# Two single PSUM banks as tiles of their own in the first sweep of a graph layer

## The chip, the cores and the metric

The kernel runs on one core of a Trainium2 chip. TensorE (PE in the profile, its weight loads PEld) multiplies into PSUM; VectorE (DVE) and ScalarE (ACT) read and write PSUM and SBUF; GpSimd (POOL) works in SBUF; SyncE (SP) issues the transfers. The metric is the device time of one execution in microseconds, as a median of several.

## The reference

For each of 64 batches there is a 256 x 768 block `x` and a 256 x 256 matrix `adj` of zeros and ones. With `h` the normalised and rectified `x`:

```
h    = max(layernorm(x), 0)
ctx  = adj @ (h @ Wadj.T) / deg  +  adj.T @ (h @ Wrev.T) / rdeg  +  h @ Wself.T      (biases left out)
rel  = (adj-weighted sums of E rows) @ Wr.T  +  the same, reversed, @ Wrr.T
out  = x + ctx + rel
```

So three products of a 256 x 768 by a 768 x 768 matrix are needed in each batch, in fp32 accuracy, and then two products with the adjacency matrix. As the entries are zeros and ones, the part `rel` comes down to a few rows added per batch.

## The kernel before

The three dense products of a batch are computed as one product of a block matrix through 15 smaller products (a scheme with fewer multiplications; the table `PRODUCTS` names them 1 to 15). Each factor is a sum or difference of column blocks of `h`, named `a0` to `b2`. To keep fp32 accuracy in TensorE's faster format, a left factor is split into three words: `left0` (ACT, line 593), `left1` (DVE, line 606) and `left2` (DVE, line 610). Weights are split alike and stay in SBUF. All 15 sets of weights don't fit there at once, so there are two sweeps over the batches: the first does products 10, 5, 2, 8, 11, 14, 3 and 13, writes its partial sums and `h` to memory, and the second does the other seven, the adjacency products and the output. Two of the 64 batches take a direct path with plain fp32 matmuls (`whole`, line 763).

A product accumulates in a chain of PSUM: in the first sweep the chains are `y`, `z` and `w`. `product` (line 627) records for each the first group of matmuls (line 621), a rescaling by ACT in place (line 655), the second group of matmuls, and reads of the sum by ACT (line 666) or DVE (lines 675 and 677). Four matmuls per word pair, 12 per product, 96 per batch in this sweep.

Nothing is issued as it is recorded. Each step is an operation with an engine, an estimated cost and a rank (a due time with a hand-set offset from a table), and `Plan.schedule` (line 301) plays the engines through in time, gives each buffer a slot of its class and writes out one order for all. `main_path` (line 1049) then emits that order. A buffer becomes a tile when its first operation is emitted: the pool, and a tag made of class and slot. A new tile under a tag waits for those that used the one before it.

[...]Class `Q` has four slots of two banks. One `Q` buffer, `hold` (line 451), lives through the whole first sweep, and its two halves, one bank each, are the two slots of class `U`. A `U` buffer is used for three things:

- `top` (line 597): in the first sweep, ACT copies `left0` of a product into it (line 600), and DVE reads it for `left1` (line 606) and `left2` (line 610). Eight a batch.
- `pt` (line 705): TensorE transposes the row statistics into it (line 707) and ACT reads them as `line` (line 710), which goes to memory and back as the broadcast `row` with which POOL (line 726) and DVE (line 730) normalise `h`. One a batch, two batches ahead.
- `right` (line 488): at the start, the weights of product 3 are summed by TensorE in it (line 495) and split into words by ACT and DVE. Four in all.

A `U` buffer gets no tile; it is a view of half of `hold`'s tile:

```
for b in sorted(o.bufs, key=lambda b: bool(b.inside)):
    if b.inside:
        b.tile = b.inside.tile[:, b.slot, :]
```

With `hold` in place the chains share the other three slots of `Q`: a batch's `y` takes the slot that the `z` of the batch before it leaves, once DVE has read `z` (line 677, `x<-z`, product 2's sum). After the first sweep the slot of `hold` is used like the others.

Of the kernel before, what the change touches and what calls it, by code (L numbers as in the profile page):

```python
# [10 lines left out]
F32 = mybir.dt.float32  # L11
# [6 lines left out]
P = 128  # L18
# [221 lines left out]
class Buf:  # L240
    def __init__(self, cls, shape, dtype, name):
        self.cls, self.shape, self.dtype, self.name = cls, shape, dtype, name
        self.ops, self.parts, self.slot, self.tile, self.inside = [], {}, None, None, None


class Op:
# [765 lines left out]
def kernel(  # L1012
# [36 lines left out]
    def main_path(main: ExitStack):  # L1049
        pool = main.enter_context(tc.tile_pool(name="pool", bufs=1))  # L1050
        dram = main.enter_context(tc.tile_pool(name="dram", bufs=3, space=bass.MemoryType.DRAM))
        keep = main.enter_context(tc.tile_pool(name="kept", bufs=1, space=bass.MemoryType.DRAM))
        psum = main.enter_context(tc.tile_pool(name="psum", bufs=1, space=bass.MemoryType.PSUM))
        plan = Plan(SLOTS)
        own = lambda name, shape, dtype: plan.buf(None, shape, dtype, name, pool.tile(shape, dtype, name=name))
        fixed = {
            "x": x_v, "xt": x_t, "adj": adj_v, "out": out_v, "e_t": e_t, "bias": bias,
            "w": (wadj_t, wself_t, wrev_t), "wr": (wr_t, wrr_t),
            "ident": ident, "ones": ones, "half": half, "dram": dram, "kept": keep,
            "flag": plan.buf(None, None, None, "flag", flag),  # L1060
            "deg": own("deg", [P, B, C, 2], F32),
            "sq": own("sq", [P, B, C], F32),
            "cols": [own(f"cols{i}", [P, P], F32) for i in range(2)],
            "halves": [[own(f"half{c}_{i}", [P, P], F32R) for c in range(C)] for i in range(2)],
            "rd": [own(f"rd{i}", [P, C, 2], F32) for i in range(2)],
        }
        for col in fixed["cols"]:
            nc.vector.memset(col.tile, 0.0)
        for half_tile in fixed["halves"][0] + fixed["halves"][1]:
            nc.vector.memset(half_tile.tile.bitcast(F32), 0.0)  # L1070
        nc.scalar.activation(half[:, :1], half[:, :1], AF.Copy)
        record(nc, plan, fixed, B, NREL)
        for o in plan.schedule():
            for b in sorted(o.bufs, key=lambda b: bool(b.inside)):
                if b.inside:
                    b.tile = b.inside.tile[:, b.slot, :]
                elif b.tile is None:
                    b.tile = (psum if b.cls == "Q" else pool).tile(b.shape, b.dtype, tag=f"{b.cls}{b.slot}", name=b.name)
            o.emit()

    def general_path(sub: ExitStack):
# [121 lines left out]
    with ExitStack() as main:  # L1203
        with tc.manual_schedule():
            main_path(main)
# [37 lines left out]
```

## Time and profile before

| what | us |
|---|---|
| median of 3 executions | 2551.55 |
| lowest, highest | 2549.71, 2552.49 |
| the profiled execution: its own time | 2551.01 |
| the profiled execution: span from first to last instruction | 2549.2 |
| busy PE, PEld | 2509.0, 2408.4 |
| busy DVE, ACT, POOL | 2134.0, 1824.7, 1300.0 |

The share of busy time speaks for the whole span; the two sweeps must be read apart. A view by windows gives busy times of a stretch. A view of waits lists which instruction stood idle until which other was done, with the total, the times and the longest. A timeline lists instructions by start and length; what stands in brackets is the time for which the engine had been idle and who ended that. A line number with the tile name is the way to find a step in the code: `hold` in a row is a half of that tile, without saying which.

### The profile page before, as it was taken

To read this page: it belongs to the slowest core of one execution; us is meant where nothing else is said; L and a number is where in the kernel's file an instruction comes from. 1 tells how busy PE (TensorE), PEld (TensorE's weight loads), DVE (VectorE), ACT (ScalarE), POOL (GpSimd) and SP (SyncE) were. 2 spreads that over 40 slices of the span, in tenths; PEclk is the share of its full clock that TensorE was granted. 3 is DMA by queue.
4 is the path that set the end of the run, shared out by engine and by line. 5 is a ranking of instruction groups with operands and counts; after the bars stand their busy time and mean duration, and the time that the engine had idled before them with its cause. 6 is when DMAs were issued, how large, how long until landed. Compare 5 with 4: busy or idle time off the path is not lost. (4 is left out here: it accounts for less than half of the span.)

```text
span 2549.2 us, 43499 instructions
## 1 busy us (share of the span) xinstructions
PE 2509.0 (98%) x13922; PEld 2408.4 (94%) x13922; DVE 2134.0 (84%) x3933; ACT 1824.7 (72%) x3901; POOL 1300.0 (51%) x1138
## 2 busy tenths in 40 slices
PE   7999999999999999999999999999999999999998
PEld 4899999999999999996999999999999999999998
DVE  7777777777777777778899999999999999999997
ACT  4788888888888888886666666666666666666664
POOL 1555555555555555542555555555555555555553
PEclk9999999999999999999999999999999999999999
DMA  5677677777777777777576666676666666666663
GB/s 210 233 275 265 254 277 262 256 277 257 262 277 261 256 279 262 269 256 253 177 217 210 210 209 212 210 216 208 212 210 211 210 212 210 212 210 211 217 211 132
DMA packets 223970, 590.63 MB, mean 232 GB/s; under 512 B 24036, under 2 KB 24292, under 8 KB 223736
## 3 DMA queue, kind: packets, MB, share of 16 engines
q1 hardware_dynamic: 223736, 587.79, 68.3%
q8 instruction: 112, 1.84, 0.3%
q14 instruction: 122, 1.00, 0.1%
HBM read 364.22 MB, written 223.48 MB: 231 GB/s over the span
## 5 line engine op out<-in xcount | busy, mean ns | idle before, releaser
L903 POOL TENSOR_TENSOR hl<-c,hl 128x768 fp32r<-128x768 f32 x256 | 490.5, 1936 | 397.7 <-ACT hl L899 344.8
L621 PE MATMUL y<-word,left 128*128 128x384 f32 x2976 | 591.1, 340 | 12.1 <-DVE x L677 7.6
L621 PE MATMUL x<-word,left 128*128 128x384 f32 x2976 | 570.7, 336 | 1.5 <-ACT x L655 1.0
L621 PEld LDWEIGHTS y<-word,left 128*128 128x128 f32 x2976 | 518.7, 188 | 40.0 <-DVE x L677 28.5
L621 PEld LDWEIGHTS x<-word,left 128*128 128x128 f32 x2976 | 520.9, 188 | 4.7 <-ACT x L655 1.6
L915 PE MATMUL agg<-hl,a 128*128 128x384 f32 x2048 | 399.0, 338 | 0.1
L915 PEld LDWEIGHTS agg<-hl,a 128*128 128x128 f32 x2048 | 355.9, 188 | 15.2 <-DVE c L677 14.7
L726 POOL TENSOR_TENSOR h<-h,row 128x768 f32<-128x768 f32 x128 | 235.6, 1861 | 221.5 <-DMA row<-d 179.7
L899 ACT ACTIVATE hl<-c 128x768 fp32r<-128x768 f32 x256 | 203.2, 839 | 155.1 <-PE agg L915 142.8
L621 PE MATMUL w<-word,left 128*128 128x384 f32 x1488 | 304.2, 339 | 0.1
L621 PE MATMUL z<-word,left 128*128 128x384 f32 x1488 | 301.4, 337 | 0.4 <-ACT left L593 0.2
L610 DVE SCALAR_TENSOR_TENSOR left<-left,hold 128x256 fp32r<-128x256 f32 x496 | 201.2, 416 | 107.9 <-ACT hold L600 103.2
L926 DVE SCALAR_TENSOR_TENSOR c<-agg,rd,c 128x768 f32<-128x768 f32 x252 | 254.0, 1008 | 28.7 <-PE agg L915 28.5
L610 DVE SCALAR_TENSOR_TENSOR left<-left 128x256 fp32r<-128x256 f32 x434 | 267.9, 640 | 0.0
L655 ACT ACTIVATE x<-x 128x768 f32<-128x768 f32 x248 | 197.4, 796 | 96.2 <-PE x L621 94.6
L621 PEld LDWEIGHTS z<-word,left 128*128 128x128 f32 x1488 | 260.1, 188 | 4.0 <-ACT c L666 0.5
L621 PEld LDWEIGHTS w<-word,left 128*128 128x128 f32 x1488 | 258.3, 188 | 3.2 <-ACT c L666 0.4
L655 ACT ACTIVATE y<-y 128x768 f32<-128x768 f32 x248 | 197.1, 795 | 51.9 <-PE y L621 51.3
L600 ACT ACTIVATE hold<-left 128x256 f32<-128x256 f32 x496 | 191.2, 385 | 37.2 <-DVE left L610 15.4
L704 POOL TENSOR_TENSOR cols<-cols,half 128x2 f32<-128x2 f32 x64 | 82.7, 1292 | 213.6 <-DVE cols L703 210.4
L675 DVE TENSOR_TENSOR c<-c,v 128x768 f32<-128x768 f32 x124 | 117.9, 951 | 81.2 <-PE v L645 79.4
L583 POOL TENSOR_TENSOR a1+a<-h 128x256 f32<-128x256 f32 x62 | 45.9, 741 | 271.8 <-DMA h<-kept_h 239.7
(137 smaller groups left out, 4438.7 us busy)
## 6 DMA issues: line engine op xcount, KB each, us to landing
c<-kept SPq DMA_DIRECT2D x316, 384.0 KB
kept<-c SPq DMA_DIRECT2D x252, 384.0 KB
x<-in_x_dram SPq DMA_DIRECT2D x128, 384.0 KB
h<-in_x_t_dram SPq DMA_DIRECT2D x128, 384.0 KB
out_dram<-c SPq DMA_DIRECT2D x126, 384.0 KB
kept_h<-h SPq DMA_DIRECT2D x124, 384.0 KB
h<-kept_h SPq DMA_DIRECT2D x124, 384.0 KB
adj<-in_adj_dram SPq DMA_DIRECT2D x64, 512.0 KB
```

The costliest lines, as they stand in the source:

```text
L583: lambda: nc.gpsimd.tensor_tensor(t(home), x[1](), y[1](), op=op),
L600: lambda: nc.scalar.activation(view(top), t(w)[:, 0].bitcast(F32), AF.Copy),
L610: lambda: nc.vector.scalar_tensor_tensor(t(w)[:, 2], t(w)[:, 1].bitcast(F32), -STEP, first(), op0=ALU.mult, op1=ALU.add), s == 1,
L621: nc.tensor.matmul(t(q)[:, half, : H // 2], t(w)[:, lw, f, :], t(r[rw])[:, f, ts(half, H // 2)], start=start and i == 0 and f == 0, stop=s ...
L655: lambda: nc.scalar.activation(view(), view(), AF.Copy, scale=scale),
L675: emit = lambda to=to, op=op: nc.vector.tensor_tensor(to(), to(), view(), op=op)
L704: pool(0.7, r - 21.5, f"pow {b}", [col], [col], lambda: nc.gpsimd.tensor_tensor(var(), var(), v["half"], op=ALU.pow))
L726: lambda h=h, one=one: nc.gpsimd.tensor_tensor(t(h), t(h), one(0), op=ALU.subtract),
L899: lambda: nc.scalar.activation(t(pair)[:, 0], t(o), AF.Copy, scale=LOWER),
L903: lambda: nc.gpsimd.tensor_tensor(t(pair)[:, 1], t(o), t(pair)[:, 0].bitcast(F32), op=ALU.subtract),
L915: nc.tensor.matmul(t(q)[:, half, : H // 2], t(s["a"])[:, c, k, ts(ic, P)], t(pairs[c])[:, part, ts(half, H // 2)], start=(c == 0 and part ...
L926: lambda q=q, to=to, ic=ic: nc.vector.scalar_tensor_tensor(to(), t(q)[:, :, : H // 2], t(rd)[:, ic, k : k + 1], to(), op0=ALU.mult, op1=AL ...
```

## The change

`hold` no longer gets a tile. A `U` buffer has a shape of its own, one bank of fp32, and gets a tile in a new pool `single` under the tag of its slot, so two tags and two banks. The planner still keeps `hold` as a buffer that reserves one slot of `Q`. When the slot is handed to another `Q` buffer later on, `single` is closed and a pool `late` is opened for the buffers of that slot. The order of the operations, the slots and the ranks are those of before.

```diff
@@ class Buf
         self.cls, self.shape, self.dtype, self.name = cls, shape, dtype, name
         self.ops, self.parts, self.slot, self.tile, self.inside = [], {}, None, None, None
+        if cls == "U":
+            self.shape, self.dtype = [P, 512], F32
@@ main_path
         psum = main.enter_context(tc.tile_pool(name="psum", bufs=1, space=bass.MemoryType.PSUM))
+        singles = ExitStack()
+        single = singles.enter_context(tc.tile_pool(name="single", bufs=1, space=bass.MemoryType.PSUM))
+        held, late = None, None
...
         for o in plan.schedule():
-            for b in sorted(o.bufs, key=lambda b: bool(b.inside)):
-                if b.inside:
-                    b.tile = b.inside.tile[:, b.slot, :]
+            for b in o.bufs:
+                if b.name == "hold":
+                    held = b.slot
                 elif b.tile is None:
-                    b.tile = (psum if b.cls == "Q" else pool).tile(b.shape, b.dtype, tag=f"{b.cls}{b.slot}", name=b.name)
+                    home = {"Q": psum, "U": single}.get(b.cls, pool)
+                    if b.cls == "Q" and b.slot == held:
+                        if late is None:
+                            singles.close()
+                            late = main.enter_context(tc.tile_pool(name="late", bufs=1, space=bass.MemoryType.PSUM))
+                        home = late
+                    b.tile = home.tile(b.shape, b.dtype, tag=f"{b.cls}{b.slot}", name=b.name)
             o.emit()
```

## The prediction

> **What bounds the kernel now.** First the windows view, cut at 76 us (first product of the first sweep), 1150 us (its last) and 1202 us (first of the second). Columns: window, length, busy us (instructions) of PE, PEld, DVE, ACT and POOL, clock, DMA share, GB/s.
>
> ```profile
> 76.00:1150.00 1074.00, 1061.36 (x5966) 1027.54 (x5965) 823.82 (x1792) 886.61 (x1786) 571.44 (x553) 1.00 0.73 265
> 1202.00:2530.00 1328.00, 1326.45 (x7516) 1299.60 (x7515) 1201.45 (x1994) 866.86 (x1991) 695.40 (x555) 1.00 0.67 209
> ```
>
> TensorE carries both sweeps. In the first its weight loads (PEld) leave 46.5 us of 1074 idle; VectorE has 250 us free and ScalarE 187. So only what shortens PE's waits counts. Next, the waits view between 80 and 1150 us for PEld and for DVE (total, times, longest), and from the view of line 677 what its DVE reads waited for, of which the line on PE's `z` is shown:
>
> ```profile
> PEld y L621 <- DVE x L677: 28.5, 59, 0.8
> PEld y L621 <- DVE c L677: 6.2, 28, 0.2
> ...
> DVE left L610 <- ACT hold L600: 102.7, 122, 1.2
> ...
> DVE left L606 <- ACT line L710: 34.7, 59, 3.8
> DVE left L606 <- ACT hold L600: 28.7, 40, 2.3
> ...
>   PE z L621: 0.3, 1
> ```
>
> PE waits once per batch, 59 times, for DVE to read product 2's sum out of `z`: the next batch's `y` takes that pair of banks, because `hold` leaves the chains only three of the four slots. The read had to wait for PE's `z` only once. So it is ready and stands in DVE's queue behind other work: lines 610 and 606, which wait for ACT for 166 us in all. One such stretch in the timeline, DVE first, then ACT, then PE (start, length, engine, operation, in brackets the idle time before and its releaser):
>
> ```profile
> 628.72 0.42 DVE L606 TENSOR_TENSOR left<-h,hold 128x256 fp32r<-128x256 f32 x1 [0.67 <-ACT line L710]
> 630.32 0.42 DVE L610 SCALAR_TENSOR_TENSOR left<-left,hold 128x256 fp32r<-128x256 f32 x1 [1.18 <-ACT hold L600]
> 630.65 0.41 DVE L606 TENSOR_TENSOR left<-b0+b,hold 128x256 fp32r<-128x256 f32 x1
> 631.59 0.42 DVE L610 SCALAR_TENSOR_TENSOR left<-left,hold 128x256 fp32r<-128x256 f32 x1 [0.52 <-ACT hold L600]
> 631.92 0.95 DVE L677 SCALAR_TENSOR_TENSOR x<-z,x 128x768 f32<-128x768 f32 x1
> ```
>
> ```profile
> 628.43 0.25 ACT L710 ACTIVATE line<-hold 4x128 f32<-4x128 f32 x1
> ...
> 629.91 0.38 ACT L600 ACTIVATE hold<-left 128x256 f32<-128x256 f32 x1
> ...
> 631.16 0.39 ACT L600 ACTIVATE hold<-left 128x256 f32<-128x256 f32 x1 [0.18 <-DVE left L606]
> ```
>
> ```profile
> 629.75 1.57 PE L621 MATMUL z<-word,left 128*128 128x384 f32 x8
> ...
> 631.68 0.72 PEld L621 LDWEIGHTS y<-word,left 128*128 128x128 f32 x4
> 632.93 0.19 PEld L621 LDWEIGHTS y<-word,left 128*128 128x128 f32 x1 [0.53 <-DVE x L677]
> ```
>
> Read it with the halves that the planner hands out. Product 13 of a batch holds one half; the other holds product 14, then the transposed column `pt`, then product 5 of the next batch. The first 606 (left1 of 13) reads 13's half, written long before, yet starts 0.04 us after `line` has read the other half: a read held up by another read, of other data. The 610 behind it (left2 of 13) waits 1.18 us for ACT's copy of product 5 into the other half. The 610 at 631.59 (left2 of 5) waits 0.52 us for the copy of product 11, again into the half that it doesn't read. So the program orders accesses by the tile, not by the half. Of DVE's waits, 102.7 us (two a batch) and 34.7 us are of this false kind; the 28.7 are mostly true, left1 of 14 waiting for its own copy.
>
> **What the Trainium skill says.** "PSUM — Partial Sum Buffer", PSUM bank collisions raise a hardware error, asks for accesses to be guarded by bank and quadrant and lets engines use different banks at once. A half of `hold` is 512 fp32 wide, one such bank, so the halves need no order between them; the trace shows an order all the same. "Perfetto Trace Analysis", Identifying the Most-Contended Engine, judges TensorE by its weight loads rather than by matmul busy time; the trace agrees, since PE's matmul rows show 7.6 us of the same wait where the weight loads show 28.5. "SBUF — State Buffer", Who interferes with whom, says that a DVE instruction with two SBUF inputs contends with GpSimd. Agreed: line 610 with `hold` never exceeds 425 ns in 496 runs, while in the second sweep, without `hold`, the same operation reaches 2079.
>
> **The change part by part.** Ranks, slots and the order on each engine come from the planner, which is not touched: no instruction or DMA of the work is added, dropped or moved, and SP's and POOL's queues keep their order. What changes is which tile an access names.
>
> (a) Each `top`, `pt` and `right` gets a tile of its own in the pool `single`, one tag per half. The false waits go: DVE's two kinds above, and ACT's for line 606 (11.1 us, 59 times, by the same view). True ones stay: a copy waits until the last reader of its own slot is through.
>
> In the stretch shown, left1 and left2 of 13 would run from about 628.1, under the wait. Left1 of 5 inherits the true wait: its copy ends at 629.91 + 0.38 = 630.29, so it starts at 630.33 and not at 630.65. Left2 of 5 follows 0.46 later (the spacing of such a pair without a wait: 625.75 and 626.21 in the same view), at 630.79, and ends at 631.21. The `z` matmuls end at 629.75 + 1.57 = 631.32. DVE starts some 0.10 us after such an end (the `w` matmuls from 617.07 take 1.55, DVE reads them from 618.72), so the read runs from 631.42 to 632.37 in place of 631.92 to 632.87. It released PE 0.06 us after its end; that becomes 632.43. PE was free to load at 631.68 + 0.72 = 632.40. The wait shrinks from 0.53 to 0.03.
>
> Over the sweep: 28.5 / 59 = 0.483 us a batch, less about 0.05, the part of such a wait in PEld that does not move the matmuls (0.53 us idle there moved them by 0.49), is 0.433 x 59 = 25.6 us. The 6.2 us behind `c<-y` I leave in: there DVE stands behind the normalisation (line 730) and left1 of 14, whose wait is true.
>
> What is late next: PE itself, 96 matmuls at 0.174 us (8 in 1.39 from run to run) or 16.7 us a batch, some 0.12 for the transpose and 0.1 for `c<-y`, against 1074 / 62 = 17.3 now. ACT needs 886.61 / 62 = 14.3 and DVE 13.3. DMA would rise from 265 to some 272 GB/s; slices of the page reach 279.
>
> (b) Fresh tiles could need more wait instructions. Line 600 has 366 event semaphores of 17 ns before 491 copies already (its view). One more for every copy is 491 x 17 ns = 8.3 us of ACT; all of them gone is -6.2. Either is hidden in ACT's 187 idle us: cost 0. If they fell in the stretch shown, 17 ns would come off a margin of 0.2.
>
> (c) `single` is closed and `late` opened once, after the last use of `hold` (1150.8 us in its view). The tile placed there waits for the same readers as now: 0, since no other wait is due. Were it to wait for the chain's end, one read and its hand-overs, 0.95 + 0.10 + 0.06 = 1.1 us, with PE busy for all of 1150 to 1202. A gain is excluded there.
>
> (d) The start: product 3's words pass through the halves between 25 and 50 us. PE's waits there (0.58 us the longest) follow ACT's word, a true step, and the rest lies under the `whole` matmuls. Bounds 0 and -2 us; I take 0.
>
> Sum: -25.6 us on the profiled execution of 2551.0 us (span 2549.2) is 2525.4. The median shown is 0.5 us above it: 2525.9.
>
> **The rivals.** *Half of it.* Another wait takes over: `c<-y` stalls in all batches and not in 28, or the row that POOL awaits by DMA (171 us of waiting in the sweep) comes late at the faster pace. For it: the planner laid the order out for 17.2 us a batch. Against: neither is a loop that closes within a batch; both shift with PE. Half the gain: 2551.5 - 12.8 = 2538.7.
>
> *Nothing.* The new tiles are still ordered against each other, or left1 of 5, truly waiting for ACT, holds back the read as much. For it: the copy at 629.91 stands behind four ACT instructions. Against: left2 of 5 then still ends 0.21 us before the read can start. 2551.5.
>
> *Slower.* DVE, running early, puts line 730, with two SBUF inputs, beside POOL's work, just ahead of `c<-y`, for which PE waits already in 28 batches. The second sweep prices one hit at 2079 - 417 (the median) = 1.66 us; 28 are 46.5, less 25.6 is +20.9: 2572.4. It decides from 16 hits on (25.6 / 1.66). Against: line 730's median is 952 ns, its longest 1525, and it is timed by PE and ACT, not by the false waits.
>
> **How the numbers follow.** The gain as worked out, -20 to -33 us: 0.68. Half: 0.19. Nothing: 0.08. Slower: 0.05. A measurement tells 0.2%, 5.1 us, from no change. Forecast and half case are faster by more: 0.87; same 0.08; slower 0.05. The low end adds the 6.2 us of `c<-y` and the start's 2: 2525.9 - 8.2 = 2517.7. The high end is the half case with (c)'s 1.1 us: 2539.8. Outside lie nothing, slower and some tails, 0.17.
>
> **What would show it.** Right: DVE's waits in lines 610 and 606 for `hold` and `line`, 166 us, fall to the true ones, some 30 of left1 of 14 and up to 1 us a batch of left1 of 5; the read of `z` waits for PE; PEld's wait for it falls below 5 us; the first sweep is some 26 us shorter, the second as long as now. Wrong: if the false waits stay, (a) fails at its root; if they go and PE's wait stays, the read was bound elsewhere; if both go and the sweep is no shorter, another row of PE's waits has grown.

## The result, and the profile after

| | before | after |
|---|---|---|
| median, us | 2551.47 | 2519.32 |
| lowest, highest | 2549.71, 2552.49 | 2519.23, 2519.53 |
| profiled execution: own time, span | 2551.01, 2549.2 | 2519.23, 2517.3 |
| after / before, with 95% interval | | 0.9875 [0.9858, 0.9892] |

The gain is 32.2 us where 25.6 were forecast: 2519.3 against 2525.9, inside the range. Of all the executions behind this document only one was slow: one of the kernel with left2 of 5 put back took 14100.65 us, and its median below leaves it out. Line numbers of the changed kernel are two higher (606 is 608, 610 is 612, 677 is 679), and the halves are now called `top`, `pt` and `right`.

The windows view of the changed kernel, cut at the same events to within 2 us (columns as in the prediction):

```profile
76.00:1118.00 1042.00, 1040.33 (x5964) 1029.88 (x5962) 822.74 (x1789) 875.54 (x1785) 570.83 (x554) 1.00 0.74 273
...
1170.00:2498.00 1328.00, 1326.68 (x7515) 1300.20 (x7514) 1201.69 (x1994) 866.67 (x1992) 695.32 (x555) 1.00 0.67 209
```

All of it is in the first sweep: 1074 us became 1042, and the second sweep has the same 1328. PE's weight loads stood idle for 46.5 us of the first sweep and now for 12.1. VectorE's idle time there went from 250 to 1042 - 822.74 = 219 us, 31 us less, which is about the 32 us by which the sweep is shorter. So VectorE does the same work in less time; the waits that it keeps stand where PE doesn't stand behind them.

The waits view of the changed kernel between 80 and 1118 us for PEld, seven entries in all, of which the first four and the last are shown:

```profile
PEld w L623 <- DVE x L776: 1.6, 1, 1.6
PEld z L623 <- ACT left L595: 0.5, 1, 0.5
PEld z L623 <- ACT c L668: 0.4, 1, 0.4
PEld y L623 <- ACT y L657: 0.4, 2, 0.2
...
PEld y L623 <- DVE x L679: 0.2, 1, 0.2
```

The wait for the read of `z`, 28.5 us in 59 batches, is down to one of 0.2. The other, 6.2 us for `c<-y`, is gone too, and that one the prediction had left in. The same view for DVE:

```profile
DVE left L608 <- ACT top L602: 96.0, 71, 2.2
DVE c L679 <- ACT top L602: 61.4, 56, 1.2
DVE left L608 <- PE w L623: 21.8, 26, 2.2
...
DVE x L679 <- PE z L623: 1.8, 10, 0.3
```

The view names what came last, and two of these rows are old waits under new names. The second is the read of `w`, which stood as 60.2 us behind PE's `w` before: ACT's copies now end at nearly the same time. The third is left1 of 14, which before was most of the 28.7 us behind ACT's copies.

Line 612, `left2`, no longer waits at all in this view, and nothing waits for `line` any more. But line 608, `left1`, waits longer for ACT's copies than line 606 did. The view by lines of the same stretch says for which product (partitions x elements; then busy us and mean ns; then idle us before it and its releaser):

```profile
L608 DVE TENSOR_TENSOR left<-b0+b,top 128x256 fp32r<-128x256 f32 x61 | 25.7, 422 | 86.9 <-ACT top L602 86.8
L608 DVE TENSOR_TENSOR left<-a0+a1+b0+b,top 128x256 fp32r<-128x256 f32 x62 | 26.1, 421 | 29.3 <-PE w L623 21.8 <-ACT top L602 5.1
```

`b0+b` is the left factor of product 5, and 86.8 / 61 = 1.42 us a batch: the true wait of left1 of 5 for its own copy. `a0+a1+b0+b` is that of product 14. The stretch of the timeline that answers to the one in the prediction, DVE, ACT, then PE's matmuls and its weight loads:

```profile
611.50 0.41 DVE L608 TENSOR_TENSOR left<-h,top 128x256 fp32r<-128x256 f32 x1
611.94 0.42 DVE L612 SCALAR_TENSOR_TENSOR left<-left,top 128x256 fp32r<-128x256 f32 x1
613.93 0.42 DVE L608 TENSOR_TENSOR left<-b0+b,top 128x256 fp32r<-128x256 f32 x1 [1.57 <-ACT top L602]
614.38 0.42 DVE L612 SCALAR_TENSOR_TENSOR left<-left,top 128x256 fp32r<-128x256 f32 x1
614.89 0.96 DVE L679 SCALAR_TENSOR_TENSOR x<-z,x 128x768 f32<-128x768 f32 x1
```

```profile
613.45 0.38 ACT L602 ACTIVATE top<-left 128x256 f32<-128x256 f32 x1
...
614.45 0.38 ACT L602 ACTIVATE top<-left 128x256 f32<-128x256 f32 x1
```

```profile
613.29 1.57 PE L623 MATMUL z<-word,left 128*128 128x384 f32 x8
```

```profile
615.22 2.11 PEld L623 LDWEIGHTS y<-word,left 128*128 128x128 f32 x12
```

Both instructions of 13 are through by 612.4, while before they ended beside PE's `z`. Left1 of 5 starts 0.10 us after its copy (613.45 + 0.38 = 613.83), left2 of 5 0.45 later, before the copy of 11 at 614.45, for which it once waited. Its end, 614.80, lies 0.06 us ahead of the end of PE's `z` (613.29 + 1.57 = 614.86), and the read follows at once and ends at 615.85. Of the 12 loads of `y` from 615.22 on, at 0.176 each, the fifth, the first into the slot that `z` leaves, starts at 615.92, just after the slot is free. Before, that run was cut into 4 and the rest by 0.53 us; here it is one run of 12.

To tell where the matmuls gained, the 13922 matmuls of the two kernels, which come in the same order in both, were laid side by side and the difference of their starts followed:

| place in the order | us gained there |
|---|---|
| `y`, at the first matmuls of product 5, behind the read of `z` | 25.4 |
| `y`, at the first matmuls of product 14, behind `c<-y`, every second batch | 3.3 |
| one wait of `y` for ACT's rescaling, once | 1.35 |
| start, net, and all the rest up to the end of the sweep | 1.4 |
| second sweep | 0.2 |

So the sum is 31.7 us, of which the read of `z` is 25.4 (25.6 in the prediction) and `c<-y` 3.3. The 28.5 and 6.2 us that PEld had shown as idle moved the matmuls by 25.4 and 3.3. "Perfetto Trace Analysis", Identifying the Most-Contended Engine, in the Trainium skill takes the busy share of the weight loads as a measure of how close TensorE is to its limit; as a price of a single wait their idle time says too much here, by a tenth in one case and nearly twofold in the other.

Why the wait for `c<-y` went shows in ACT's timeline, before and then after, where ACT copies the words of products 13 and 14 into the two halves one after the other (x2: two instructions shown as one). Both stretches are of a batch of the kind that stalled, in which a normalisation stands between left1 of 14 and `c<-y`:

```profile
607.51 0.80 ACT L600 ACTIVATE hold<-left 128x256 f32<-128x256 f32 x2
```

```profile
625.33 0.69 ACT L602 ACTIVATE top<-left 128x256 f32<-128x256 f32 x2
```

The pair took 0.80 us and takes 0.69: two copies into different banks, by the same engine, were held apart by 0.11 us. Left1 of 14 waits for the second, and the normalisation and `c<-y` come behind it. No idle time of ACT shows this: the two now overlap, and before they stood end to end.

What each instruction awaits can be read in the program as well. A listing of the semaphores that each of five DVE instructions of one batch awaits, before and after:

```
                    before                       after
left1 of 13   DMA, Activation              DMA
left2 of 13   Activation                   DVE
left1 of 5    DMA, Pool                    DMA, Activation, Pool
left2 of 5    Activation                   DVE
x <- z        PE                           PE
```

(`Activation` is ACT, `Pool` is POOL.) Left2 of 13 awaited ACT for a copy of another product. A listing for the kernel before with `hold` as one flat tile of 1024 columns, cut by columns, has the same waits as the kernel before; it was not run. So, as far as these listings go, it is the common tile that makes the order, and not the form of the view; the first experiment tests it on the chip.

### The profile page after: what moved, and what is told of

It is laid out like the page before. It is cut to its first block, busy times and chain, and to the rows that moved or that the text cites. A ratio compares the mean times of both kernels' runs of the same rounds, so it can differ in the third digit from the quotient of the medians.

```text
span 2517.3 us, 43767 instructions
## 1 busy us (share of the span) xinstructions
PE 2489.2 (99%) x13922; PEld 2412.2 (96%) x13922; DVE 2134.8 (85%) x3933; ACT 1814.3 (72%) x3901; POOL 1300.7 (52%) x1138
## 5 line engine op out<-in xcount | busy, mean ns | idle before, releaser
L623 PE MATMUL y<-word,left 128*128 128x384 f32 x2976 | 573.2, 337 | 0.0
L917 PEld LDWEIGHTS agg<-hl,a 128*128 128x128 f32 x2048 | 356.0, 188 | 15.0 <-DVE c L679 14.5
L928 DVE SCALAR_TENSOR_TENSOR c<-agg,rd,c 128x768 f32<-128x768 f32 x252 | 252.8, 1003 | 28.7 <-PE agg L917 28.5
L612 DVE SCALAR_TENSOR_TENSOR left<-left,top 128x256 fp32r<-128x256 f32 x496 | 199.8, 413 | 6.4
L602 ACT ACTIVATE top<-left 128x256 f32<-128x256 f32 x496 | 181.3, 383 | 6.0 <-DVE left L612 2.0
```

What stands on the lines that cost most here:

```text
L602: lambda: nc.scalar.activation(view(top), t(w)[:, 0].bitcast(F32), AF.Copy),
L612: lambda: nc.vector.scalar_tensor_tensor(t(w)[:, 2], t(w)[:, 1].bitcast(F32), -STEP, first(), op0=ALU.mult, op1=ALU.add), s == 1,
L623: nc.tensor.matmul(t(q)[:, half, : H // 2], t(w)[:, lw, f, :], t(r[rw])[:, f, ts(half, H // 2)], start=start and i == 0 and f == 0, stop=s ...
L917: nc.tensor.matmul(t(q)[:, half, : H // 2], t(s["a"])[:, c, k, ts(ic, P)], t(pairs[c])[:, part, ts(half, H // 2)], start=(c == 0 and part ...
L928: lambda q=q, to=to, ic=ic: nc.vector.scalar_tensor_tensor(to(), t(q)[:, :, : H // 2], t(rd)[:, ic, k : k + 1], to(), op0=ALU.mult, op1=AL ...
```

## The experiments

The theory: in the kernel before, accesses to the two halves are ordered as if to one, and of these waits only those count that stand in DVE's queue right ahead of what PE awaits, the read of `z`. Rivals: that the gain comes from the fresh tile for every buffer (more of them, and a pool closed early); that it comes in proportion to the waiting removed, wherever it stood; and that it comes from the copies of ACT.

### Is it the fresh tiles: two tiles for the whole sweep

```diff
+        pair = {}
...
+                elif b.cls == "U":
+                    if b.slot not in pair:
+                        pair[b.slot] = single.tile([P, 512], F32, tag=f"U{b.slot}", name=f"half_bank{b.slot}")
+                    b.tile = pair[b.slot]
```

> The changed kernel, but each half is one tile for the whole first sweep in place of a fresh tile per buffer. Theory (the order was kept by the tile, so it is enough that the halves are two tiles): within 2 us of the changed kernel, 2519 us. Rival (the gain comes from the fresh tiles and the way a slot is handed on): a good part of the 32 us is lost, 2530 us or more.

Measured: 2517.89 us (2517.2 to 2518.84), ratio to before 0.9865 [0.9849, 0.9881]. Two tiles that stay give the whole gain. What counts is that there are two, not that each buffer has a new one.

### Single waits put back

In the changed kernel an operation is made to wait for another, through a table of pairs: the operation `one` of a batch also waits for `two` of the batch that stands `ahead` further on. Data and order stay as they are.

```diff
+AGAIN = (("left2 5", "top 11", 0),)
...
-            o.emit()
+            done[o.name] = o.emit()
+            kind, _, last = o.name.rpartition(" ")
+            for one, two, ahead in AGAIN:
+                other = done.get(f"{two} {int(last) + ahead}") if kind == one else None
+                if other is not None:
+                    tc.add_manual_dep(
+                        done[o.name].ins, other.ins.name,
+                        mybir.DependencyInfo(mybir.DependencyClass.Sync, mybir.DependencyReason.DATA), reason="again",
+                    )
```

The tables of four kernels with one kind of wait each (`top` is ACT's copy of a product, `left1` and `left2` its words on DVE), and of one with all of them:

```diff
+AGAIN = (("left2 5", "top 11", 0),)
...
+AGAIN = (("left2 13", "top 5", 1),)
...
+AGAIN = (("left1 13", "line", 2),)
...
+AGAIN = (("top 14", "top 13", 0), ("top 8", "top 3", 0))
...
+AGAIN = (("left2 5", "top 11", 0), ("left2 13", "top 5", 1), ("left1 13", "line", 2), ("top 14", "top 13", 0), ("top 8", "top 3", 0), ("top 11", "left1 5", 0))
```

Left2 of 5 behind the copy of 11:

> The changed kernel with one false wait put back by hand: left2 of product 5 waits for ACT's copy of product 11. Theory (only what delays the read of z counts): in the changed kernel that copy ends at 614.83 us and left2 of 5 starts at 614.38; put back, the read starts 0.3 us later and PE waits 0.25 to 0.3 us in 61 batches, so +15 to +18 us, 2534 to 2537 us. Rival (all false waits count by their length: this one is about 32 of 166 us): +6 us, 2525 us.

Left2 of 13 behind the copy of the next batch's 5:

> The changed kernel with another false wait put back: left2 of product 13 waits for ACT's copy of product 5. Theory: the longest of the false waits (1.2 us a batch, some 72 us) costs little, as left1 of 5 waits for the same copy anyway; the read of z comes 0.1 us later, of which 0.03 to 0.08 reach PE: +2 to +5 us, 2521 to 2524 us. Rival (by length): 72 of 166 us of the gain, +14 us, 2533 us.

Left1 of 13 behind `line`:

> The changed kernel with the third false wait put back: left1 of product 13 waits until ACT has read the transposed column. Theory: it lies wholly under the wait of left1 of 5 for its own copy, so 0 to +1 us, 2519 to 2520 us. Rival (by length, 34.7 of 166 us): +6.7 us, 2526 us.

The copies of a pair behind each other:

> The changed kernel in which ACT's copies of 14 and 8 each wait again for ACT's copy just before (13 and 3). Theory: left1 of 14 comes 0.1 us later, and in every second batch the read of y behind it too, which PE awaits there; that is the 3.3 us of the gain which the matmul starts show at c<-y: +2 to +4 us, 2521 to 2523 us. Rival (the gain at c<-y comes from DVE's other false waits): 0, 2519 us.

All of them, and the copy of 11 behind left1 of 5:

> The changed kernel with six false waits put back together: left2 of 13 after the copy of 5, left2 of 5 after the copy of 11, left1 of 13 after the read of the transposed column, the copy of 11 after left1 of 5, and the copies of 14 and 8 each after the copy just before it (13 and 3). Theory: this is nearly all that stood in the way of PE before, so 2546 to 2550 us, within 5 us of the kernel before; PE's wait for the read of z is back at 0.45 us a batch or more. Rival (something else about the tiles or the layout of the banks gave the gain): 2540 us or less.

Measured, against the 2519.3 of the changed kernel:

| put back | median, us | ratio to before | over the changed kernel |
|---|---|---|---|
| left2 of 5 | 2530.84 | 0.9916 [0.9897, 0.9936] | 11.5 |
| left2 of 13 | 2520.4 | 0.9875 [0.9858, 0.9891] | 1.1 |
| left1 of 13 | 2517.87 | 0.9866 [0.985, 0.9883] | -1.4 |
| the copies | 2521.98 | 0.9884 [0.9868, 0.9901] | 2.7 |
| all | 2547.8 | 0.9986 [0.9979, 0.9993] | 28.5 |

A difference of about 1 us can't be told here: over the sessions of this document the kernel before had medians between 2551.5 and 2552.3. Left2 of 5 cost less than the 15 to 18 us of its theory, though more than the 6 of the rival; left2 of 13 came out below its 2 to 5; left1 of 13 lies 1.4 us below the changed kernel, of which 1.0 stands in its trace before the first product of the sweep. The copies and all six together came out as expected. By the starts of the matmuls, left2 of 5 costs 12.7 us at the read of `z`; 1.4 come back at PE's single wait of 1.6 us (the first row of PEld's view above), which is missing in that trace.

Now the waits, in the waits views of the first sweep. With left2 of 5 put back, DVE and then PEld:

```profile
DVE left L613 <- ACT top L603: 30.5, 59, 0.5
```

```profile
PEld y L624 <- DVE x L680: 15.7, 58, 0.6
```

With left2 of 13 put back, DVE, and the first two entries of PEld:

```profile
DVE left L613 <- ACT top L603: 109.7, 59, 2.3
```

```profile
PEld w L624 <- DVE x L777: 1.6, 1, 1.6
PEld y L624 <- ACT y L658: 0.5, 3, 0.2
```

With left1 of 13 put back, DVE:

```profile
DVE left L609 <- ACT line L713: 34.2, 58, 1.0
```

109.7 us of waiting, put back, cost 1.1 us; 34.2 cost nothing that can be told; 30.5 cost 11.5. The two cheap ones stand ahead of left1 of 5, which waits for its own copy anyway: DVE stands there 1.4 us a batch, under whatever name. So most of the 109.7 is not new: left1's own row falls from 96.0 to 9.2 us with it, while it stays at 94.1 with left2 of 5. Counted with that row, DVE waits some 23 us more than in the changed kernel in the first case and some 29 more in the second, for 1.1 and 11.5 us. The rival of proportion falls with this, by length as the view gives it and by what was added. Left2 of 5 stands between that wait and the read of `z`. The timeline of the same place, DVE and PE's `z`, with left2 of 13 put back and then with left2 of 5:

```profile
614.63 0.42 DVE L613 SCALAR_TENSOR_TENSOR left<-left,top 128x256 fp32r<-128x256 f32 x1 [1.95 <-ACT top L603]
614.97 0.41 DVE L609 TENSOR_TENSOR left<-b0+b,top 128x256 fp32r<-128x256 f32 x1
615.42 0.42 DVE L613 SCALAR_TENSOR_TENSOR left<-left,top 128x256 fp32r<-128x256 f32 x1
615.76 0.95 DVE L680 SCALAR_TENSOR_TENSOR x<-z,x 128x768 f32<-128x768 f32 x1
...
614.06 1.57 PE L624 MATMUL z<-word,left 128*128 128x384 f32 x8
```

```profile
619.28 0.42 DVE L609 TENSOR_TENSOR left<-b0+b,top 128x256 fp32r<-128x256 f32 x1 [1.56 <-ACT top L603]
620.22 0.42 DVE L613 SCALAR_TENSOR_TENSOR left<-left,top 128x256 fp32r<-128x256 f32 x1 [0.52 <-ACT top L603]
620.56 0.95 DVE L680 SCALAR_TENSOR_TENSOR x<-z,x 128x768 f32<-128x768 f32 x1
...
618.64 1.57 PE L624 MATMUL z<-word,left 128*128 128x384 f32 x8
```

PE's `z` ends at 615.63 in the first and at 620.21 in the second, so the read starts 0.13 and 0.35 us behind it; in the changed kernel it was 0.03. The first shows the room that there is. A read that waits for nothing follows left2 of 5 after 0.34 us, while in the changed kernel, held by PE's `z`, it came after 0.51: 0.17 to spare. One more instruction behind the copy moves left1 of 5 from 0.10 to 0.37 us after the copy's end (614.60); of these 0.27 the room takes 0.17, and 0.10 reach the read, of which PE had 0.07 to spare (615.85 to 615.92 in the changed kernel). In the second kernel the 0.52 us of waiting come behind left1 of 5, and 0.32 of them reach the read.

With the copies put back, and with all put back, the first entries of PEld's waits:

```profile
PEld y L624 <- DVE c L680: 6.2, 28, 0.2
```

```profile
PEld y L624 <- DVE x L680: 28.2, 59, 0.8
PEld y L624 <- DVE c L680: 6.2, 28, 0.2
PEld w L624 <- DVE x L777: 1.6, 1, 1.6
```

The wait for `c<-y` comes back whole, 6.2 us in 28 batches, by the order between ACT's copies alone (those of 14 and 8 behind those of 13 and 3; which of the two pairs counts was not run apart), and costs 2.7 us. With all, both of the old kernel's waits are there to within 0.3 us, and the time is 3.7 us short of the old one, although the tiles, their pools and their places are those of the changed kernel: at most those 3.7 us of the gain can come from where the tiles lie. By the starts of the matmuls the 28.4 that it loses are 25.1 at the read of `z` and 3.25 at `c<-y`. Of the 3.3 that remain by that count 1.35 is the single wait for a rescaling named above; the rest, at the start and in single places, was not put back and is not settled.

### Two and three of them: a sum or a chain

The parts make 11.5 + 1.1 + 0 + 2.7 = 15.3 us, all together 28.5. The copy of 11 behind left1 of 5 had been tried only with all the rest. Two kernels tell whether the missing 13 us lie in it.

```diff
+AGAIN = (("left2 5", "top 11", 0), ("left2 13", "top 5", 1))
...
+AGAIN = (("left2 5", "top 11", 0), ("left2 13", "top 5", 1), ("top 11", "left1 5", 0))
```

> The changed kernel with two false waits put back: left2 of 13 after the copy of 5, and left2 of 5 after the copy of 11. Alone they cost 1.4 and 11.5 us. Theory (a chain, not a sum): with the first, left1 of 5 ends at 614.62 us and not at 614.35, still before the copy of 11 ends (614.83), for which left2 of 5 waits in any case: as with the second alone, +11 to +14 us, 2530 to 2533 us. Rival (what all six cost together, 28 us, comes from these two): 2540 us or more.

> The same two, and a third: the copy of 11 waits for left1 of 5. Theory: now the three are links of one chain: left1 of 5 ends at 614.62, the copy of 11 runs from 614.66 to 615.04 and left2 of 5 starts at 615.08, 0.2 us later than with two: another 12 us, +23 to +27 us, 2542 to 2546 us. The read of the transposed column has no part in it. Rival (the third adds nothing, and the order of the copies or the transposed column is what is missing to the six): 2533 us or less.

Measured: 2532.2 us, 0.9921 [0.9905, 0.9938], with two, which is 12.9 over the changed kernel: the sum of their parts (12.6) to within what can be told. And 2548.03, 0.9985 [0.9978, 0.9992], with three, which is 28.7 over it and 2 us above the range that was expected. So the third link is worth 15.8 us where the two others are present. Left2 of 13 waits for the copy of 5, so left1 of 5 comes behind left2 of 13; the copy of 11 waits for left1 of 5; and left2 of 5 waits for the copy of 11. With every link the lateness goes through the whole chain and out at the read of `z`; with the middle link missing, ACT copies 11 early and left2 of 5 finds it nearly done. That left2 of 13 is needed for this was not run apart; it follows from the times in the changed kernel, where left1 of 5 ends at 614.35 us, before the copy of 11 starts at 614.45, so that the third link alone would hold up nothing there.

The three cost as much as all, without the wait for `c<-y`. PEld's first entry with three:

```profile
PEld y L624 <- DVE x L680: 31.3, 59, 0.8
```

31.3 us stand here where it was 28.2 with all. The likely reason is that PE, not held at `c<-y` in half of the batches, comes to the read of `z` that much earlier and waits there. So the copies' 2.7 us are worth something only once the chain is gone: three links cost 28.7, and all six 28.5.

### The place in DVE's queue: the same work ahead of the read and behind it

One extra DVE instruction a batch, a sum over data that nobody uses, right ahead of the read of `z` and right behind it.

```diff
+        filler = main.enter_context(tc.tile_pool(name="filler", bufs=1)).tile([P, 1], F32, name="filler")
...
+            if o.name.startswith("read 2 "):
+                nc.vector.tensor_reduce(filler, ident.unsqueeze(1).to_broadcast([P, 4, P]), AX.XY, ALU.add)
             o.emit()
```

In the second kernel the two added lines stand behind `o.emit()`.

> The changed kernel with one more DVE instruction a batch in the first sweep, a sum over 512 elements (some 0.6 us), directly ahead of the read of z. Theory: the read has hardly any slack; it comes some 0.4 us later, and PE waits 0.3 to 0.4 us in 61 batches: +18 to +25 us, 2538 to 2544 us. Rival (DVE's time in the sweep counts, wherever it stands: 62 x 0.6 = 37 us of more work): the same as with the instruction behind the read.

> The changed kernel with the same additional DVE instruction directly behind the read of z. Theory: it falls into time that DVE has to spare: 0 to +2 us, 2519 to 2521 us. Rival (DVE's total time counts): the same cost as ahead of the read.

Measured: 2538.53 us, 0.9947 [0.993, 0.9964], ahead of it, 19.2 over the changed kernel; 2519.21, 0.9873 [0.9856, 0.9889], behind it, no change, although DVE is busy for 858.37 us of the sweep in place of 822.74. The timeline with the extra work ahead, DVE, then PEld:

```profile
624.78 0.42 DVE L612 SCALAR_TENSOR_TENSOR left<-left,top 128x256 fp32r<-128x256 f32 x1
625.12 0.68 DVE L1092 TENSOR_REDUCE filler<-ident 128x1 f32<-128x512 f32 x1
625.72 0.95 DVE L679 SCALAR_TENSOR_TENSOR x<-z,x 128x768 f32<-128x768 f32 x1
```

```profile
626.72 1.36 PEld L623 LDWEIGHTS y<-word,left 128*128 128x128 f32 x8 [0.39 <-DVE x L679]
```

The read starts 0.94 us after left2 of 5; it was 0.51 in the changed kernel (614.38 to 614.89). Of the instruction's 0.68 us 0.43 reach the read, since the read follows it after 0.60 and the room of 0.17 ahead of the read goes first, and PE waits 0.39: nearly all that reaches the read reaches PE. 19.2 / 59 is 0.33 a batch in the end. This is the price of time at that place, with nothing of tiles in it.

### The same reading in the second sweep

In the changed kernel PE's largest wait of the second sweep is one for DVE:

```profile
PEld agg L917 <- DVE c L679: 14.5, 58, 0.4
```

Ahead of that read in DVE's queue stands left1 of product 15. Two kernels move work away from there. The first puts left1 of 15 behind the read of product 1. The second puts it just ahead of left2 of 15, which is behind the first read of `agg`, and puts left2 of 4 behind the second read of `agg`.

```diff
+            if kind == "left1 15" and 3 <= int(last) <= 61:
+                waiting.append(o)
+                continue
             o.emit()
+            if kind == "read 1":
+                while waiting:
+                    waiting.pop(0).emit()
```

```diff
+            if kind in ("left1 15", "left2 4") and 3 <= int(last) <= 61:
+                waiting[kind] = o
+                continue
+            if kind == "left2 15" and "left1 15" in waiting:
+                waiting.pop("left1 15").emit()
             o.emit()
+            if kind == "agg11" and o.eng == "DVE" and "left2 4" in waiting:
+                waiting.pop("left2 4").emit()
```

> The changed kernel with one step moved in the second sweep: left1 of product 15 is issued on DVE behind the read of product 1 (line 679, c<-x) and no longer four instructions ahead of it, in 59 batches. PE waits for that read before the second group of agg in 58 batches, 14.5 us by its weight loads. Theory (the same reading as in the first sweep: what counts is what stands in DVE's queue ahead of the read that PE awaits): the read starts 0.2 us earlier, when the matmuls of x are done, and PE gets most of the 11.9 us back that its matmul starts show there: -9 to -12 us, 2507 to 2510 us. Rival (the wait only moves on, to the transpose behind agg or to the first product of the next batch, since left1 of 15 now stands ahead of the degree steps and the read of agg): 0, 2519 us.

> The changed kernel with two steps moved in the second sweep: left1 of product 15 stands behind the first read of agg (ahead of left2 of 15) and left2 of product 4 behind the second read of agg. Moving left1 of 15 alone brought nothing, as the reads of agg then came 0.12 us later and PE waited for them, at the transpose and at u. Theory: now the read of product 1 starts 0.2 us earlier and both reads of agg no later than in the changed kernel, so none of the three waits is left: -8 to -12 us, 2507 to 2511 us. Rival (DVE has no room left in that stretch, and the wait moves on again): 2517 to 2521 us.

Measured: 2520.79 us, 0.9876 [0.986, 0.9893], in the first; 2553.83, 1.0006 [0.9998, 1.0014], in the second. Both theories missed; the first came out about where its rival had it, the second far above both. PEld's waits in the second sweep of the first:

```profile
PEld u L623 <- DVE c L928: 10.6, 59, 0.3
PEld pt L886 <- DVE c L928: 10.2, 58, 0.2
```

The wait at line 917 is gone and two others stand in its place, together longer: 20.8 us for 14.5. The work that left one read's way is in the way of two. By the starts of the matmuls 11.5 us are gained at `agg`, as hoped, and as much is lost behind it. In the second, PE's waits and then PEld's (`issue`: the profile shows nothing that ended the wait), and a stretch of DVE:

```profile
PE v L647 <- DVE c L677: 20.9, 59, 0.6
```

```profile
PEld v L647 <- issue: 32.7, 51, 0.9
PEld u L623 <- DVE c L928: 13.1, 57, 0.3
```

```profile
1713.16 1.15 DVE L612 SCALAR_TENSOR_TENSOR left<-left 128x256 fp32r<-128x256 f32 x1
1714.24 0.94 DVE L677 TENSOR_TENSOR c<-c,v 128x768 f32<-128x768 f32 x1
```

Left2 of 4 now stands ahead of the read of `v` that product 7 awaits, and it takes longer there: 1.15 us in the median of 59 batches, for 0.41 in the changed kernel. In all 59 an `hl` instruction of GpSimd (line 905) runs beside it, in the changed kernel in hardly any batch; that GpSimd is what stretches it was not tested apart. By the starts of the matmuls 10.7 us are gained at `agg`, but 34.8 are lost at the rows of product 7 and 9.9 at product 15. In the second sweep DVE is busy for 1201.69 of 1328 us, and neither place that was tried is one behind which nobody waits; in the first, with 219 idle, there was one.

No version that beats the changed kernel was found: the two that lie 1.4 us below it are within what can be told.

## Why the prediction was right, point by point

**(a), the waits by tile.** Right at its root: the waits of left2 of 13 and 5 and of left1 of 13 for other products' copies are gone, and with them PE's wait for the read of `z`, at 25.4 us of matmul starts against 25.6. The stretch worked out by hand came out in its order: left1 of 5 behind its own copy, left2 of 5 just before the end of PE's `z`, the read just behind that end. The margin of left2 of 5 was forecast at 0.21 us and is 0.09 (614.80 to 614.89), or 0.17 if one counts from when the read could have started: left1 of 5 came 0.10 us after its copy where 0.04 had been taken, and the read 0.03 after PE's `z` where 0.10 had been. Of the 34.7 us that the prediction calls false, 3.8 are a single wait of left1 of 14, which doesn't touch the sum.

The term that was mis-sized is `c<-y`, "the 6.2 us behind `c<-y` I leave in". Its reason, that left1 of 14 has a true wait, holds, but the copy for which it waits was itself held up by the copy of 13, a false order on ACT that shows as no idle time. It measured 3.3 us of matmul starts, and 2.7 when put back alone. The low end of the range had included it; without it the result would have been outside.

**(b), more wait instructions.** There are 268 more instructions in the trace: event semaphores such as those ahead of line 602 in the first sweep, 454 of 17 ns in place of 367, and ahead of line 608, 318 of mostly 21 ns in place of 278. Cost 0, as taken; PE's weight loads are idle for 12 us of the sweep, and the waits view puts none of it down to these.

**(c), the change of pools.** 0, as taken: PE is busy in 51.98 of the 52 us between the sweeps.

**(d), the start.** 0 taken, bounds 0 to -2. The first product starts 1.7 us earlier, of which 1.4 is given back within the first batch: 0.3 net. With the single wait of 1.35 us for ACT and some 1.1 in small places this makes the rest of the gap between 25.6 and 31.7.

**The rivals.** *Half*: no other wait took the place; PEld's view has no row for `c<-y`, and the transfers run at 273 GB/s where 272 had been worked out. *Nothing*: its mechanism is there, left1 of 5 does wait for ACT 1.42 us a batch, but the read comes behind it in time, as the point against it said. *Slower*: line 732 (then 730) has a median of 952 ns as before and a longest of 1568 where it was 1525. "SBUF — State Buffer", Who interferes with whom, in the Trainium skill names such a hit as possible beside a GpSimd instruction that reads SBUF; in the whole run two of the 128 take over 1.1 us, where 16 hits were needed.

**What would show it.** One sign was wrong though the time was right: DVE's waits were to fall from 166 us to some 30 and at most 1 us a batch. They fell to 96.0 + 21.8 = 118 us at line 608. Left1 of 14 kept 27 us, near the 30 forecast; the waits removed from 13 reappear at left1 of 5, where 1.4 us a batch is a true wait for ACT. They are not a cost: DVE is early, and idles there in place of further back.

## What to carry to other kernels

Two halves of one tile were ordered here as one thing, even a read after a read and a copy after a copy on the same engine; where the parts have lives of their own, give them tiles of their own. Price a wait not by its length but by what stands behind it in the same queue: start from the read that the busiest engine awaits and go up its queue until the first true wait, for what lies ahead of that cost little here. Put back alone, the parts of such a chain may cost far less than all of it (11.5 and 1.1 here, and 28.7 with the link between them), so try them together too. And an instruction that is moved need not keep its length: left2 of 4 went from 0.4 to 1.15 us.

## What was not expected of the hardware

A wait between two instructions of one engine can be there without idle time to show it: two copies of ACT took 0.80 us as a pair in place of 0.69, and only the 2.7 us at another engine told of it. And 30.5 us of waiting right before the read cost ten times as much as 109.7 a few instructions further up the queue, most of which the next instruction would have waited anyway.
